# Dividing the x products anew over the eight steps of a block in a gated RNN kernel

## The chip, the cores and the metric

The kernel runs on one core of a Trainium2 chip. The metric is the device time of one execution in microseconds (us). PE is TensorE, DVE is VectorE, ACT is ScalarE, POOL is GpSimd and SP is SyncE; PEld is the part of TensorE that loads weights.

## What is computed

The reference is a gated recurrent cell over 512 time steps, with batch 8 and 512 units, all in float32, and the input added to the result:

```python
def step(h, x_t):
    fused = sigmoid(concatenate([x_t, h]) @ w_W + w_b)
    hidden_state, output_state = split(fused, 2)
    memory_state = x_t @ wx_W + wx_b + hidden_state * (h @ wh_W + wh_b)
    return output_state * h + (1.0 - output_state) * tanh(memory_state)
out = x + scan(step, cond, x)
```

Every step needs the h of the step before it. The products with x don't: they can be made ahead of time.

## The kernel before

**One step.** The loop over i (512 steps) writes out, in the order in which each engine will run them, all instructions of a step; no scheduler moves them. PE first runs the recurrent products of h with its weights. `ORDER` names them: A0 A1 A2 A3, then D0 to D3, then H2 H3. A letter is a PSUM tile (A has 256 columns for the first half of h and 192 for the second, D has 128, H has 64), a digit is a quarter of the 512 values of h. A0 and A1 read the first half of h (tile hTA), A2 and A3 the second (hTB). Each is a loop of four matmuls over j (the calls of `mm`, line 195). Such a matmul has 32 columns of weights (h or x of a few steps is the stationary operand) and writes to a strip of 32 partitions, so that four of them, one for each strip, run beside each other. A float32 matmul is two matmul instructions in the trace, each with its weight load. I call four matmul instructions on the four strips a **round**: a product of four matmuls is two rounds.

**The chain of a step.** When A is complete, DVE transposes its gate values (`tr`, L415; md1A, L430; `tz`, L415), ACT takes the sigmoids (L226), DVE runs a scan that makes the memory state (`m`, L403), ACT takes the tanh, and a second DVE scan writes the new h (`update`, L403), first for hTA, later for hTB. A0 of the next step waits for the first, A2 for the second.

**The x products.** After the recurrent products of step i, PE does one share of the x products of a later block: `take(later, 1)` resumes the generator `products(o)` until its next `yield`. A block o is eight steps, i = 8o to 8o + 7, and I write **u** for i modulo 8. The x products of two groups of four steps are made together with sums and differences of x and of the weights (p1, p2, p3, p4, p6, p7 and `shared`, after Strassen's way to multiply), from i = 4 on, and so for 62 blocks (o = 2 to 63). `pair(left, right, k, c0, c1)` is four matmuls of columns c0 to c1 of 384; `shared(k)` is four of 192 columns. The `yield` statements cut them into shares. There is none at the end of `products`, so that the last piece of one block and the first of the next are in one share. This is how columns fall on steps before the change:

| step u | pieces, in columns of four matmuls each | sum |
|---|---|---|
| 0 | 320 (p4, p3) | 320 |
| 1 | 64 (p4, p3), 192 (shared), 64 (p4, p3) | 320 |
| 2 | 192 (shared), 128 (p4, p3) | 320 |
| 3 | 192 (p4, p3), 128 (p1, p7 of the next block) | 320 |
| 4 | 256 (p1, p7), 64 (p1, p7) | 320 |
| 5 | 320 (p1, p7) | 320 |
| 6, 7 | 384 (p2, p6) | 384 |

**Beside it.** DVE and ACT also move the finished x products from PSUM (xp) to SBUF and into the start values of A, D and H, some work in each step after the updates (lines 526 to 585), and POOL adds x to the output (L595) and makes the sums of x (L294).

Of the kernel before, what the change touches and what calls it, by code (L numbers as in the profile page):

```python
# [48 lines left out]
def tile_cond_rnn_residual(  # L49
# [144 lines left out]
    def mm(out_, lhsT, rhs, start=False):  # L194
        nc.tensor.matmul(  # L195
            out_, lhsT, rhs, start=start, stop=False, skip_group_check=True
        )
# [69 lines left out]
    def wx_of(kh, nh):  # L267
        return wx[:, 2 * kh : 2 * kh + 2, 2 * nh : 2 * nh + 2]

    def x_half(o, n, kh):  # L270

        return x_of(o // 2, slice(2 * kh, 2 * kh + 2), 8 * (o % 2) + GS * n, GS)
# [23 lines left out]
    def products(o):  # L296

        t_ = [q[o % 2] for q in sx]
        p1 = (0, x_half(o, 0, 0), wx_of(0, 0))
        p2 = (0, x_half(o, 0, 1), wx_of(1, 0))  # L300
        p3 = (0, t_[3], wx_of(1, 1))
        p4 = (1, x_half(o, 1, 1), tw[3])
        p6 = (0, t_[1], tw[1])
        p7 = (1, t_[2], tw[2])

        def pair(left, right, k, c0=0, c1=WIDE):
            for j in range(NQ):
                bank, lhs, rhs = left if j < 2 else right
                mm(
                    xps[bank][32 * j : 32 * j + 32, COLS.start + c0 : COLS.start + c1],  # L310
                    lhs[:, k],
                    rhs[:, k, j % 2, c0:c1],
                    start=right is p7 and k == 0 and c0 == 0 and j >= 2,
                )

        def shared(k):
            for j in range(NQ):
                c0 = HALF * (1 - j // 2)
                mm(
                    xps[j // 2][32 * j : 32 * j + 32, COLS.start : COLS.start + HALF],  # L320
                    t_[0][:, k],
                    tw[0][:, k, j % 2, c0 : c0 + HALF],
                )

        pair(p1, p7, 0, 0, 128)
        if o > 2:
            yield
        pair(p1, p7, 0, 128)
        pair(p1, p7, 1, 0, 64)
        yield  # L330
        pair(p1, p7, 1, 64)
        yield
        pair(p2, p6, 0)
        yield
        pair(p2, p6, 1)
        yield
        pair(p4, p3, 0, 0, 320)
        yield
        pair(p4, p3, 0, 320)
        shared(0)  # L340
        pair(p4, p3, 1, 0, 64)
        yield
        shared(1)
        pair(p4, p3, 1, 64, 192)
        yield
        pair(p4, p3, 1, 192)

    def take(it, n=None):
        while n is None or n > 0:
# [4 lines left out]
    def x_side():  # L354
        for o in range(2, NG // 2):
            yield from products(o)
# [337 lines left out]
```

## Time and profile before

| | |
|---|---|
| median of 3 runs | 1657.46 us (1657.08 to 1657.48) |
| the profiled execution, its own time | 1659.18 us |
| its span, from the first to the last instruction | 1657.4 us |
| granted TensorE clock | 1.000 |
| PE busy | 1646.6 us (99%) |
| PEld busy | 1295.7 us (78%) |
| DVE busy | 1439.3 us (87%) |
| ACT busy | 1137.5 us (69%) |
| POOL busy | 328.5 us (20%) |

Matmuls are pipelined and the ends that the trace gives for them are modelled, so that a busy PE is not a PE without pauses: pauses of some tens of ns do not show as idle time. The starts are recorded. In the timeline a row is a group of like instructions: its start in us from the start of the span, its length in us, the engine, the line, the operation, the tile written and those read, the shape, and a count; behind it, in brackets, the idle time before it and what ended it.

### The profile page before, as it was taken

What the parts mean: (1) busy time and instruction counts of PE and PEld (TensorE: products, weight loads), DVE (VectorE), ACT (ScalarE), POOL (GpSimd) and SP (SyncE); (2) the same over time, 40 slices, a digit from 0 to 9 for tenths busy, and PEclk for the clock granted to TensorE, in tenths of its full rate; (3) what the DMA queues carried; (4) which work ended last, traced back from release to release, by engine and by line L of the source; (5) the groups of instructions that cost most, each with busy time, mean ns of one, the idle gap of its engine ahead of it and who ended that gap; (6) DMA issues with size and microseconds to landing.
All of it is one profiled execution on the core that took longest, in us unless ns stands there. A gap on an engine that the chain in (4) does not pass through costs nothing.

```text
span 1657.4 us, 114239 instructions
## 1 busy us (share of the span) xinstructions
PE 1646.6 (99%) x47566; PEld 1295.7 (78%) x47566; DVE 1439.3 (87%) x11237; ACT 1137.5 (69%) x5884; POOL 328.5 (20%) x1290
## 2 busy tenths in 40 slices
PE   9999999999999999999999999999999999999998
PEld 5778777787777777777877777778777777787776
DVE  6888888888888888888888888888888888888887
ACT  3667767677677676676776766767767667677665
POOL 2221121211211212112112121121121211211211
PEclk9999999999999999999999999999999999999999
DMA  4000000000000000000000000000000000000000
GB/s 180 17 5 17 17 17 17 10 11 17 17 17 17 5 17 17 17 17 4 18 17 17 17 13 9 17 18 17 17 5 18 17 17 17 4 17 10 11 11 10
DMA packets 11472, 30.41 MB, mean 18 GB/s; under 512 B 1220, under 2 KB 1732, under 8 KB 10952
## 3 DMA queue, kind: packets, MB, share of 16 engines
q1 hardware_dynamic: 10800, 22.94, 4.1%
q8 instruction: 372, 6.09, 1.6%
q14 instruction: 148, 1.21, 0.2%
q10 hardware_dynamic: 152, 0.16, 0.0%
HBM read 14.70 MB, written 8.39 MB: 14 GB/s over the span
## 4 chain that ended last, share of the span: by engine, by line
PE 97%; DVE 2%; issue 0%; ACT 0%; DVEq 0%
PE A L195 47%; PE D L195 26%; PE xp L195 18%; PE H L195 7%; DVE m L403 0%; DVE tr L415 0%; DVE md1B L472 0%; DVE tw L283 0%; DVE md1A L430 0%; DVE hTA L403 0%; DVE tz L415 0%; DVE hTA L167 0%; DVE hTB L167 0%; DVE hTB L403 0%; DVE md1B L430 0%
## 5 line engine op out<-in xcount | busy, mean ns | idle before, releaser
L195 PE MATMUL A<-wa,hTA 128*32 128x256 f32 x8176 | 535.6, 379 | 2.8 <-DVE hTA L403 2.7
L195 PE MATMUL A<-wa,hTB 128*32 128x192 f32 x8176 | 430.8, 328 | 0.0
L195 PEld LDWEIGHTS A<-wa,hTA 128*32 128x32 f32 x8176 | 270.0, 122 | 166.0 <-DVE hTA L403 81.6
L595 POOL TENSOR_TENSOR ot<-xin,hTB 128x16 f32<-128x16 f32 x503 | 125.1, 249 | 1287.6 <-DVE hTB L403 1276.9
L195 PEld LDWEIGHTS A<-wa,hTB 128*32 128x32 f32 x8176 | 258.1, 123 | 133.4 <-DVE hTB L403 103.5
L195 PE MATMUL D<-wd,hTB 128*32 128x128 f32 x8192 | 317.9, 273 | 0.0
L195 PE MATMUL D<-wd,hTA 128*32 128x128 f32 x8192 | 317.8, 273 | 0.0
L226 ACT ACTIVATE md0A<-tr 128x16 f32<-128x16 f32 x512 | 112.7, 220 | 242.0 <-DVE tr L415 229.6
L195 PE MATMUL xp<-tw,sx 128*32 128x192 f32 (+5 forms) x2480 | 276.3, 358 | 0.0
L195 PEld LDWEIGHTS D<-wd,hTA 128*32 128x32 f32 x8192 | 257.8, 122 | 20.8
L415 DVE STREAM_TRANSPOSE tr<-A 128x64 f32<-128x64 f32 x511 | 127.9, 250 | 147.6 <-PE A L195 138.6
L195 PEld LDWEIGHTS D<-wd,hTB 128*32 128x32 f32 x8192 | 240.7, 122 | 0.0
L226 ACT ACTIVATE hTB<-m 128x8 f32<-128x8 f32 x1024 | 163.4, 208 | 89.2 <-DVE m L403 85.7
L195 PE MATMUL xp<-wx,xin 128*32 128x384 f32 (+4 forms) x1552 | 219.2, 384 | 0.0
L195 PE MATMUL H<-wa,hTB 128*32 128x64 f32 x8192 | 208.5, 219 | 0.0
L195 PEld LDWEIGHTS H<-wa,hTB 128*32 128x32 f32 x8192 | 186.1, 122 | 0.0
L226 ACT ACTIVATE hTB<-hTB 128x16 f32<-128x16 f32 x512 | 121.1, 236 | 85.6 <-DVE hTB L403 84.7
L403 DVE TENSOR_TENSOR_SCAN hTA<-hd0A,hTA 128x24 f32<-128x24 f32 x1024 | 175.9, 172 | 0.0
L403 DVE TENSOR_TENSOR_SCAN hTB<-hd0B,hTB 128x24 f32<-128x24 f32 x1024 | 154.6, 193 | 21.8
L226 ACT ACTIVATE hTA<-m 128x8 f32<-128x8 f32 x1024 | 161.1, 206 | 2.3
L403 DVE TENSOR_TENSOR_SCAN m<-md0B,md1B 128x24 f32<-128x24 f32 x1024 | 154.7, 193 | 2.0
L403 DVE TENSOR_TENSOR_SCAN m<-md0A,md1A 128x16 f32<-128x16 f32 x1024 | 142.3, 181 | 8.6
(104 smaller groups left out, 2725.3 us busy)
## 6 DMA issues: line engine op xcount, KB each, us to landing
xin<-in_x_dram SPq DMA_DIRECT2D x31, 256.0 KB, 3.4
out_dram<-ot SPq DMA_DIRECT2D x31, 256.0 KB, 2.2
wx<-in_wx_dram SPq DMA_DIRECT2D x4, 768.0 KB, 7.0
wa<-in_wa_dram SPq DMA_DIRECT2D x4, 512.0 KB, 9.7
wd<-in_wd_dram SPq DMA_DIRECT2D x1, 768.0 KB
wd<-in_wd_dram SPq DMA_DIRECT2D x1, 256.0 KB, 11.2
out_dram<-ot SPq DMA_DIRECT2D x1, 192.0 KB, 3.3
head<-in_xh_dram ACTq DMA_DIRECT2D x1, 144.0 KB, 5.0
```

Of the source, the lines that this page charges most:

```text
L195: nc.tensor.matmul(out_, lhsT, rhs, start=start, stop=False, skip_group_check=True)
L226: inst = nc.scalar.activation(out_, in_, func, **kw).ins
L403: return nc.vector.tensor_tensor_scan(*[t_[:, :, c_].rearrange("p n c s -> p (n c s)") for t_ in (out_, d0, d1)], 0.0, ALU.mult, ALU.add,).ins
L415: inst = nc.vector.transpose(t_.rearrange("p c n -> p (c n)"), raw[n][hf]).ins
L595: return engine.tensor_tensor(ot[:, t, 2 * hf : 2 * hf + 2, :].rearrange("p c n -> p n c"), x_of(c, slice(2 * hf, 2 * hf + 2), t, 1).rearr ...
```

## The change

Only the widths at which four of the six pairs are cut are changed. No product is added or left out, no instruction is added, and the order of the pieces stays. The sums of columns by step, from u = 0 to 7, go from 320, 320, 320, 320, 320, 320, 384, 384 to 344, 304, 328, 304, 312, 328, 384, 384. The pieces of step 1 become 40, 192 and 72, those of step 2 become 192 and 136, those of step 3 become 176 and 128, those of step 4 become 256 and 56.

```diff
         pair(p1, p7, 0, 128)
-        pair(p1, p7, 1, 0, 64)
+        pair(p1, p7, 1, 0, 56)
         yield
-        pair(p1, p7, 1, 64)
+        pair(p1, p7, 1, 56)
         yield
         pair(p2, p6, 0)
         yield
         pair(p2, p6, 1)
         yield
-        pair(p4, p3, 0, 0, 320)
+        pair(p4, p3, 0, 0, 344)
         yield
-        pair(p4, p3, 0, 320)
+        pair(p4, p3, 0, 344)
         shared(0)
-        pair(p4, p3, 1, 0, 64)
+        pair(p4, p3, 1, 0, 72)
         yield
         shared(1)
-        pair(p4, p3, 1, 64, 192)
+        pair(p4, p3, 1, 72, 208)
         yield
-        pair(p4, p3, 1, 192)
+        pair(p4, p3, 1, 208)
```

## The prediction

> **What bounds the kernel now.** I read the head of the page and its chain of waits, then the groups of matmuls by shape, then the timeline of PE over one block of eight steps, and last the weight loads that wait for h.
>
> ```profile
> span 1657.4 us, 114239 instructions
> PE 97%; DVE 2%; issue 0%; ACT 0%; DVEq 0%
> ```
>
> The chain that ends last is PE in 97% of the span. So what counts is PE's stream, and pauses in it too short to show as idle time. Here is block 32 (steps 256 to 263), by the starts of its groups, with x products where they give a price:
>
> ```profile
> 838.23 1.05 PE L195 MATMUL A<-wa,hTA 128*32 128x256 f32 x16
> 839.75 0.62 PE L195 MATMUL D<-wd,hTA 128*32 128x128 f32 x16
> 840.62 0.41 PE L195 MATMUL H<-wa,hTB 128*32 128x64 f32 x16
> 840.84 0.44 PE L195 MATMUL xp<-tw,xin 128*32 128x320 f32 x2
> 841.11 0.44 PE L195 MATMUL xp<-tw,xin 128*32 128x320 f32 x2
> 841.38 1.04 PE L195 MATMUL A<-wa,hTA 128*32 128x256 f32 x16
> 842.94 0.62 PE L195 MATMUL D<-wd,hTA 128*32 128x128 f32 x16
> 844.58 1.05 PE L195 MATMUL A<-wa,hTA 128*32 128x256 f32 x16
> 845.45 0.83 PE L195 MATMUL A<-wa,hTB 128*32 128x192 f32 x16
> 846.10 0.62 PE L195 MATMUL D<-wd,hTA 128*32 128x128 f32 x16
> 847.74 1.05 PE L195 MATMUL A<-wa,hTA 128*32 128x256 f32 x16
> 849.27 0.62 PE L195 MATMUL D<-wd,hTA 128*32 128x128 f32 x16
> 850.91 1.05 PE L195 MATMUL A<-wa,hTA 128*32 128x256 f32 x16
> 854.06 1.05 PE L195 MATMUL A<-wa,hTA 128*32 128x256 f32 x16
> 857.21 1.05 PE L195 MATMUL A<-wa,hTA 128*32 128x256 f32 x16
> 858.74 0.62 PE L195 MATMUL D<-wd,hTA 128*32 128x128 f32 x16
> 860.48 1.05 PE L195 MATMUL A<-wa,hTA 128*32 128x256 f32 x16
> 863.74 0.83 PE L195 MATMUL A<-wa,hTA 128*32 128x256 f32 x12
> ```
>
> Two things are to be seen. First, a round's time goes by its columns: H is four rounds of 64 columns in 840.84 - 840.62 = 0.22 us, 55 ns each; 320 columns take 0.27 us a round. That is (270 - 55) / 256 = 0.84 ns a column and about 2 ns on top, and x columns are two rounds, so 1.67 ns for a column of a piece and 4 to 5 ns for a piece. Second, the part of a step from A0 to D0, in which no x product lies, isn't always the same: 1.52 us in step u = 0 (839.75 - 838.23) and u = 2, but 1.56 in u = 1, 1.53 in u = 3 and u = 6. The tile's durations give that excess in ns, one row for each of the windows of u = 1, 2, 3 and 6:
>
> ```profile
> L195 PE MATMUL A<-wa,hTB x16: 326/326/365, 842.2 to 842.8; 128*32 128x192 f32 x16
> L195 PE MATMUL A<-wa,hTB x16: 326/326/326, 845.4 to 846.0; 128*32 128x192 f32 x16
> L195 PE MATMUL A<-wa,hTB x16: 326/326/350, 848.6 to 849.1; 128*32 128x192 f32 x16
> L195 PE MATMUL A<-wa,hTB x16: 326/326/342, 858.1 to 858.6; 128*32 128x192 f32 x16
> ```
>
> The columns are the shortest, the median and the longest. The first round of A2 is stretched by 39 ns in u = 1, by 24 in u = 3 and by 16 in u = 6: PE pauses there, 79 ns in the 25.51 us of this block. What it waits for is in the rows of the weight loads:
>
> ```profile
> 842.25 0.51 PEld L195 LDWEIGHTS A<-wa,hTB 128*32 128x32 f32 x16 [0.29 <-DVE hTB L403]
> 845.38 0.54 PEld L195 LDWEIGHTS A<-wa,hTB 128*32 128x32 f32 x16 [0.22 <-DVE hTB L403]
> 848.58 0.51 PEld L195 LDWEIGHTS A<-wa,hTB 128*32 128x32 f32 x16 [0.27 <-DVE hTB L403]
> 851.71 0.53 PEld L195 LDWEIGHTS A<-wa,hTB 128*32 128x32 f32 x16 [0.22 <-DVE hTB L403]
> 854.86 0.53 PEld L195 LDWEIGHTS A<-wa,hTB 128*32 128x32 f32 x16 [0.22 <-DVE hTB L403]
> 858.05 0.51 PEld L195 LDWEIGHTS A<-wa,hTB 128*32 128x32 f32 x16 [0.26 <-DVE hTB L403]
> ```
>
> In every step the load of the second half of h waits for the DVE scan; mostly it is early enough. A2's slot is 0.87 us after A0 (845.45 - 844.58). In u = 1 the load starts exactly at the slot (842.25 = 841.38 + 0.87) and the pause is 39 ns, so the matmul follows the load by 40 ns, and the load must stand at A0 + 0.825 us or earlier. It stands 0.87 after A0 in u = 1, 0.84 in u = 3 and u = 6: late. It stands 0.80 in u = 2, 4 and 5: 20 to 30 ns to spare. Over the run:
>
> ```profile
> L195 PE MATMUL A<-wa,hTB 128*32 128x192 f32 x7536 | 396.6, 328 | 0.0
> ```
>
> The mean is 328 ns over 7536 instructions, four to a round, against 326: (328 - 326) x 7536 / 4 = 3.8 us of pauses between 100 and 1600 us (2.8 to 4.7 with the rounding), 0.064 us for each of 59 blocks, within reach of the 0.079 of the one that I read.
>
> **The change part by part.** The instructions of the two programs stand in the same order with the same count on every engine; only PE's widths differ. DVE, ACT, POOL and SP issue the same work, no DMA moves, and no semaphore wait is added. Sum of columns: 2688 a block before and after; pieces: 13 before and after. So PE's own work is the same, and the change can only move pauses. By 1.67 ns a column, A0 of the next step comes later by 24 columns = 40 ns after u = 0, by 13 after u = 2 and u = 5, earlier by 27 after u = 1 and u = 3, by 13 after u = 4. The chain to the next hTB starts at this step's own A and doesn't see the x products behind it, so a longer share moves the slot away from a late load, and a shorter one moves it towards it.
>
> - **u = 1 (39 ns now).** The share before it grows by 40 ns: pause 0 to 4.
> - **u = 3 (24 here).** u = 2 grows by 13: about 11 here. The mean of all blocks must be lower than this one (64 against 79): I take 5.
> - **u = 6 (16 here).** u = 5 grows by 13: 3.
> - **u = 2 (spare 25).** u = 1 gets shorter by 27, and its own pause of 39 goes as well, 66 in all. Is the load then 40 late? That depends on whether the chain of u = 1 starts earlier by the pause that has gone. Step 9 is also a u = 1, with a longer pause:
>
> ```profile
> 51.11 1.09 PE L195 MATMUL A<-wa,hTA 128*32 128x256 f32 x16
> 52.73 0.62 PE L195 MATMUL D<-wd,hTA 128*32 128x128 f32 x16
> 55.17 0.38 PEld L195 LDWEIGHTS A<-wa,hTB 128*32 128x32 f32 x12 [0.22 <-DVE hTB L403]
> ```
>
> D starts 1.62 after A0 there and the next load 4.06 after A0; in step 257 it is 1.56 and 4.00 (845.38 - 841.38). 60 ns more pause, 60 ns later: the chain follows the end of A. So 39 of the 66 cancel, 27 are used of a spare of 25: pause 0 to 4, and the upper bound, if the chain stays where it is, is about 38.
> - **u = 4 (spare 25).** u = 3 is shorter by 27, and its pause by 13 to 19, which cancels as above: 0 to 3.
> - **u = 5 (spare 25).** 13 used: nothing. u = 7 and u = 0 stand behind the shares of 384 and don't change.
> - **A0's own wait for hTA.** In u = 1 the four loads of A0 stood after the last x round; in the shorter steps they may begin with it, 0.05 us and more before A0, and the trace's shortest lead is 40 ns. Nothing.
> - **The narrow pieces.** No row shows a round under 64 columns. 40 columns by 0.84 ns are 36 ns a round, 56 are 49. If the matmul must follow its weight load by 40 ns also in a running stream, and the load starts with the round before it, a 40-column round takes 40 to 42 ns and delays the next load too: 6 to 12 ns a block. Lower bound 0 (the linear price; below it nothing speaks). Upper bound: 55 ns a round as for 64 columns, 2 x 19 + 2 x 6 = 50 ns a block. I take 9, near the lower end, since the 40 ns is a row about these very loads.
>
> A rule speaks for that upper bound. The Trainium skill, "TensorE: Matmul & The Clock Gate", section "Back-to-back issue gap", gives 1 to 64 columns one price, about 60 cycles, an issue floor of 25 ns. Read by columns, that would make the gain 0.7 us in place of 3.2. The trace doesn't bear the floor out for one matmul: H's 16 matmuls start within 0.22 us, 14 ns apart. The same page's section "LDWEIGHTS (loading the stationary operand)" gives columns / 1.2 ns for a load, 27 ns for 32 columns; by that a 40-column round is not held up, and the sum would be 3.8 us instead.
>
> **Sum.** Pauses now 76 a block (between 64 and 79, near the one that I read in ns), afterwards 4 + 2 + 5 + 1 + 3 = 15, so 61 less; minus 9 for narrow rounds is 52 ns. 62 blocks x 0.052 = 3.2 us. The profiled execution took 1659.18 us at a span of 1657.4; the unprofiled median is 1657.46. The steps are the same in both, so the difference carries over: 1657.46 - 3.2 = **1654.3 us**, 0.19% faster.
>
> **The rivals.**
>
> 1. *The chain takes the place of the pause.* The load for u = 2 stays at 4.00 us after A0 of u = 1, because another row than A's end holds the chain (DVE's extra work in u = 1, a scan that waits for ACT). Then u = 2 pauses 38 where u = 1 did: the gain is 61 - 34 - 9 = 18 ns a block, 1.1 us, 1656.3. If u = 4 does the same, it is nothing, 1657.6. Against it: step 9.
> 2. *Rounds under 64 columns cost what 64 cost.* The gain is 61 - 50 = 11 ns, 0.7 us, 1656.8. For it: no narrower round runs now. Against it: 40 ns from load to matmul is well under 55. The skill's row for 1 to 64 columns, weighed above, is this rule.
> 3. *Slower: weight loads set the pace of narrow rounds.* One pair of rows shows a matmul that took longer than its columns:
>
> ```profile
> 2.25 0.31 PE L195 MATMUL D<-none 128*128 128x128 bf16 x1
> 2.36 0.26 PE L195 MATMUL H<-none 128*128 128x64 bf16 x1
> 2.43 0.40 PE L195 MATMUL A<-none 128*128 128x256 bf16 x1
> ```
>
> 128 columns took 0.11 us until the next start, 64 took 0.07, not half. If a round of 40 and one of 56 cost 73 ns, four such rounds add 2 x 37 + 2 x 24 = 122 ns a block; against 61 saved that is 61 x 62 = 3.8 us, 1661.2. It is slower from 61 ns of added cost on. Against it: these loads have 128 columns and ours 32, and the 64-column rounds of H already run at 55.
> 4. *No narrow cost at all:* 1653.7, the lower end.
>
> That the change does something else than it says is excluded by the order of the programs.
>
> **How the numbers follow.** About 0.2%, 3.3 us, is what a measurement of this kernel can tell from no change. My forecast with its terms (gain 2.7 to 3.8 us): chance 0.66, with rival 4 as its far end; it straddles the bound, and just over half of it is on the near side, because 9 ns for the narrow rounds puts it there. Rival 1: 0.12. Rival 2: 0.12. Rival 3: 0.06. Left for what I don't see, either sign: 0.04. Faster by over 0.2%: 0.32 of the forecast's 0.66, nothing of rivals 1 and 2, and 0.02 of the rest, 0.34; slower 0.06 + 0.02 = 0.08; the remainder, 0.58, is within. The range goes from 1653.6 (no narrow cost, pauses all gone) to 1657.2 (rival 2 and most of rival 1); about 2 in 10 are left out.
>
> **What would show it.** In the profile after: the longest A<-wa,hTB matmul of u = 1 back at 326 to 330, of u = 3 and u = 6 at 326 to 335; the mean of its group 326 to 327; no new stretch in u = 2 or u = 4 (rival 1 would show 360 there). The distance between starts of the two 40-column rounds of u = 1: 36 to 42 ns (rival 2: 55, rival 3: 73). A block of 25.45 us instead of 25.50. I am wrong if the chain of u = 1 doesn't move with A's end, or if a row outside PE changes.

## The result and the profile after

The changed kernel takes 1654.87 us (median of 22 runs, 1654.60 to 1656.29) against 1657.44 us before (22 runs). The ratio is 0.9984, with a 95% interval of 0.9978 to 0.9991: 2.57 us or 0.16% faster. Predicted were 1654.3 us and 0.19%. The interval leaves out a ratio of 1, so 0.16% could be told from no change here, less than the 0.2% that the prediction took as the least.

The head of the page after, and its chain by engine:

```profile
span 1653.0 us, 114239 instructions
...
PE 97%; DVE 2%; DMA 1%; issue 0%; ACT 0%; DVEq 0%
```

PE sets the end as before. Rows of block 31 (steps 248 to 255) from the timeline of PE: A0 of u = 0 to 4, D0 of u = 0 to 2, and one half of the rounds of the narrow piece of u = 1:

```profile
809.98 1.05 PE L195 MATMUL A<-wa,hTA 128*32 128x256 f32 x16
811.50 0.62 PE L195 MATMUL D<-wd,hTA 128*32 128x128 f32 x16
813.17 1.05 PE L195 MATMUL A<-wa,hTA 128*32 128x256 f32 x16
814.68 0.62 PE L195 MATMUL D<-wd,hTA 128*32 128x128 f32 x16
815.78 0.20 PE L195 MATMUL xp<-tw,xin 128*32 128x40 f32 x2
815.82 0.21 PE L195 MATMUL xp<-tw,xin 128*32 128x40 f32 x2
816.30 1.05 PE L195 MATMUL A<-wa,hTA 128*32 128x256 f32 x16
817.83 0.62 PE L195 MATMUL D<-wd,hTA 128*32 128x128 f32 x16
819.48 1.05 PE L195 MATMUL A<-wa,hTA 128*32 128x256 f32 x16
822.61 1.05 PE L195 MATMUL A<-wa,hTA 128*32 128x256 f32 x16
```

From A0 to D0 it is now 1.51 us in u = 1 (814.68 - 813.17), where it was 1.56, and 1.53 in u = 2, where it was 1.52. The long pause has gone and a small one has come. In ns, by the durations of A<-wa,hTB (shortest, median, longest) in the windows of u = 1, 2, 3, 4 and 6 of this block:

```profile
L195 PE MATMUL A<-wa,hTB x16: 326/326/326, 814.0 to 814.5; 128*32 128x192 f32 x16
L195 PE MATMUL A<-wa,hTB x16: 326/326/337, 817.2 to 817.7; 128*32 128x192 f32 x16
L195 PE MATMUL A<-wa,hTB x16: 326/326/326, 820.3 to 820.9; 128*32 128x192 f32 x16
L195 PE MATMUL A<-wa,hTB x16: 326/326/337, 823.5 to 824.0; 128*32 128x192 f32 x16
L195 PE MATMUL A<-wa,hTB x16: 326/326/329, 829.8 to 830.3; 128*32 128x192 f32 x16
```

0, 11, 0, 11 and 3 ns. Blocks differ: in block 32, the one that the prediction read, u = 1 keeps 21 ns, and u = 2, 3, 4 and 6 have 2, 0, 6 and 11:

```profile
L195 PE MATMUL A<-wa,hTB x16: 326/326/347, 839.5 to 840.0; 128*32 128x192 f32 x16
```

That is an exception: by the starts, 54 of 59 steps of u = 1 pause for 2 ns or less. Over 100 to 1600 us the mean of this group fell from 328 to 327:

```profile
L195 PE MATMUL A<-wa,hTB 128*32 128x192 f32 x7544 | 394.3, 327 | 0.0
```

For means over many steps I use the recorded starts: the length of a block is A0 of step 488 less A0 of step 24, over 58 blocks; a pause is the mean time from A0 to D0 over 59 steps of the same u, less 1513.4 ns, which is this mean in u = 0, 5 and 7, where PE doesn't pause. Here are the two ends for the profile before, for a second profile of the kernel before (a run described below) and for the changed kernel, each kernel's two rows in a fence of its own:

```profile
99.03 1.05 PE L195 MATMUL A<-wa,hTA 128*32 128x256 f32 x16
...
1577.70 1.05 PE L195 MATMUL A<-wa,hTA 128*32 128x256 f32 x16
```

```profile
97.69 1.05 PE L195 MATMUL A<-wa,hTA 128*32 128x256 f32 x16
...
1575.81 1.04 PE L195 MATMUL A<-wa,hTA 128*32 128x256 f32 x16
```

```profile
97.60 1.05 PE L195 MATMUL A<-wa,hTA 128*32 128x256 f32 x16
...
1573.40 1.05 PE L195 MATMUL A<-wa,hTA 128*32 128x256 f32 x16
```

That is 25.494, 25.485 and 25.445 us a block. All kernels, in ns, the sum over all eight u:

| kernel | block | pause u = 1, 2, 3, 4, 6 | sum |
|---|---|---|---|
| before, first profile | 25494 | 40, 0, 15, 0, 15 | 69 |
| before, second profile | 25485 | 38, 0, 6, 0, 15 | 59 |
| the change | 25445 | 1, 9, 1, 4, 5 | 20 |
| the change, two more profiles | 25447, 25451 | 1 to 2, 9 to 10, 0 to 2, 4 to 7, 5 to 6 | 21, 25 |
| u = 0 and 1 alone (p1_alone) | 25470 | 1, 23, 7, 0, 15 | 45 |
| u = 2 and 3 alone (p2_alone) | 25479 | 35, 0, 0, 3, 16 | 54 |
| u = 4 and 5 alone (p3_alone) | 25473 | 37, 0, 7, 0, 3 | 47 |
| over | 25481 | 1, 48, 0, 3, 4 | 55 |
| relieve | 25487 | 37, 0, 8, 0, 17 | 61 |
| relieve_div | 25438 | 5, 2, 1, 0, 4 | 13 |
| trim | 25437 | 1, 5, 1, 1, 4 | 11 |
| best | 25440 | 3, 1, 3, 2, 5 | 14 |

In every row the block less its pauses is 25425 to 25426 ns: PE's own work, which the change doesn't touch. The time went out of the pauses. (In best and in one of the "two more profiles" a single step of u = 3 pauses for 110 and 92 ns, which makes up about 2 ns of its sum; why is open.)

### The profile page after: what moved, and what is told of

Same layout as the page of the kernel before. It is cut to its first block, busy times and chain, and to the rows that moved or that the text cites. A ratio compares the mean times of both kernels' runs of the same rounds, so it can differ in the third digit from the quotient of the medians.

```text
span 1653.0 us, 114239 instructions
## 1 busy us (share of the span) xinstructions
PE 1640.8 (99%) x47566; PEld 1291.2 (78%) x47566; DVE 1438.5 (87%) x11237; ACT 1136.4 (69%) x5884; POOL 328.7 (20%) x1290
## 4 chain that ended last, share of the span: by engine, by line
PE 97%; DVE 2%; DMA 1%; issue 0%; ACT 0%; DVEq 0%
PE A L195 47%; PE D L195 26%; PE xp L195 17%; PE H L195 7%; DMA wd<-in_wd_dram 1%; DVE m L403 0%; DVE tr L415 0%; DMA rows<-in_bias_dram 0%; DVE md1B L472 0%; DVE tw L283 0%; DVE md1A L430 0%; DVE hTA L403 0%; DVE tz L415 0%; DVE hTB L403 0%; DVE md1B L430 0%
```

## The experiments

My theory: PE never rests but for pauses in front of A2, whose weight load waits for the second half of h; the division moves A2's slot against that load and nothing else, and the chain to the next load follows the end of A. Rivals: the chain doesn't follow, so that a pause only moves on; narrow rounds are dear; the gain has another source.

**Three of the four moved cuts, one at a time.** The change moves four cuts, which lie in three of the six pairs. Each edit here is against the kernel before, and blocks are compared with its second profile:

```diff
-        pair(p4, p3, 0, 0, 320)
+        pair(p4, p3, 0, 0, 344)
...
-        pair(p4, p3, 0, 320)
+        pair(p4, p3, 0, 344)
```

> Step u = 0 gets 344 columns, u = 1 gets 40 + 192 + 64 = 296, all others as before. Pauses theory (only the pauses in front of A2 change, and the chain follows the end of A): the pause of u = 1 goes from 41 ns to 0 to 2; u = 2, whose slot comes 40 + 41 earlier while its chain starts 41 earlier, gets a pause of about 15; u = 3 keeps 0 to 18 and u = 6 its 14. A block saves 28 to 46 ns, the kernel 1.7 to 2.9 us, 1654.6 to 1655.7. Rival, the chain stays where it is: the pause of u = 2 is 55, nothing is saved, 1657.4. Rival, narrow rounds are dear: the two 40-column rounds of u = 1 start 55 ns apart or more and A0 of u = 2 is later by that.

Measured: 1656.64 us against 1657.30 beside it (ratio 0.9997, interval 0.9988 to 1.0006), 14 ns a block. Two windows of A<-wa,hTB, of u = 1 and u = 2 in block 31:

```profile
L195 PE MATMUL A<-wa,hTB x16: 326/326/327, 814.8 to 815.3; 128*32 128x192 f32 x16
L195 PE MATMUL A<-wa,hTB x16: 326/326/347, 817.9 to 818.4; 128*32 128x192 f32 x16
```

The 24 columns take the pause of u = 1 away wholly, as expected, and u = 2 gets one: 23 ns in the mean, where I expected 15 and the rival 55. The chain follows the end of A, but lands some 8 ns later than that. The time saved missed its range (0.7 us for 1.7 to 2.9), because I counted from the 69 to 76 ns of the first profile and not from the 59 of the second, and by these 8 ns.

```diff
-        pair(p4, p3, 1, 64, 192)
+        pair(p4, p3, 1, 64, 208)
...
-        pair(p4, p3, 1, 192)
+        pair(p4, p3, 1, 208)
```

> Only the cut between u = 2 and u = 3 is moved: u = 2 gets 192 + 144 = 336, u = 3 gets 176 + 128 = 304. No round is under 64 columns. Pauses theory: u = 1 keeps its 41 ns, the pause of u = 3 (18 before) goes to 0, u = 4 gets 0 to 5, u = 6 keeps 14: 13 to 18 ns a block, 0.8 to 1.1 us, 1656.3 to 1656.6. Rival, columns moved change nothing: 1657.4.

Measured: 1657.05 us (0.9998, 0.9989 to 1.0007), 6 ns a block and not 13 to 18, so that the time missed its range too. The pause of u = 3 is 0, and u = 4 has 3. The pause that it takes away was 15 in the first profile of before, from which I had the 18, but it is 6 to 8 in the four others with the same pieces in u = 2 and 3 (before again, p1_alone, p3_alone, relieve). And 3 of the 6 ns lie in u = 1, which this cut doesn't touch.

```diff
-        pair(p1, p7, 1, 0, 64)
+        pair(p1, p7, 1, 0, 56)
...
-        pair(p1, p7, 1, 64)
+        pair(p1, p7, 1, 56)
```

> Only the cut between u = 4 and u = 5 is moved: 256 + 56 and 328. Pauses theory: the pause of u = 6 goes from 14 to 16 ns to 2 to 4, u = 5 stays without one: 11 ns a block, 0.7 us, 1656.7. Rival, narrow rounds are dear (the 56-column rounds at 55 ns or more in place of 49): 1656.9 to 1657.4, and the starts of these two rounds show it.

Measured: 1656.50 us (0.9995, 0.9986 to 1.0004), 12 ns a block; the pause of u = 6 is 3. As the pauses theory has it. Its two rounds of 56 columns start 49 ns apart in each of 58 blocks (49 to 50), the price by columns and not the rival's 55.

None of the intervals of these three runs can tell its kernel from the one before; the pauses in the traces do.

The three save 14 + 6 + 12 = 32 ns of the whole's 40. The rest fits the fourth cut, from 64 to 72, which was not run alone: with it u = 1 keeps 304 columns and not the 296 of p1_alone, A2's slot in u = 2 comes 13 ns later, and its pause is 9 and not 23.

**Too much of it.** 24 columns more from u = 1 to u = 2 in the changed kernel:

```diff
-        pair(p4, p3, 1, 0, 72)
+        pair(p4, p3, 1, 0, 48)
...
-        pair(p4, p3, 1, 72, 208)
+        pair(p4, p3, 1, 48, 208)
```

> The changed kernel with 24 more columns moved from u = 1 to u = 2: u = 1 has 40 + 192 + 48 = 280, u = 2 has 192 + 160 = 352. Pauses theory: the slot of u = 2 comes 40 ns earlier, its pause rises from about 8 to 41 to 48, u = 3 loses its last ns; 27 to 33 ns a block more than the changed kernel, 1.7 to 2.0 us, 1656.6 to 1656.9. Rival, the gain of the change doesn't come from these pauses: as the changed kernel, 1654.9, since all columns are there and no piece is added.

Measured: 1657.39 us against 1657.30 (1.0002, 0.9993 to 1.0010): the whole gain is gone, with the same columns and as many pieces. A block is 36 ns longer than the changed kernel's (27 to 33 expected), and the time lies over its range. The window of u = 2 in block 31:

```profile
L195 PE MATMUL A<-wa,hTB x16: 325/326/367, 818.6 to 819.2; 128*32 128x192 f32 x16
```

The slot was moved by 40 ns, and the mean pause grew by 39, from 9 to 48. The gain of the change comes from these pauses: the rival that seeks it elsewhere falls.

**The late h itself.** Instead of moving columns, I tried to make h of u = 0 earlier, with the widths of before:

```diff
-                nc.scalar.copy(u2[Q23], xps[0][Q23, COLS])
+                inst = nc.scalar.copy(u2[Q23], xps[0][Q23, COLS]).ins
+                tc.add_manual_dep(inst, spread_d.name, SYNC)
```

(`spread_d` is the copy into D of u = 5.)

> The kernel before with its widths, but in u = 0 the sigmoid that makes sz no longer carries a second wait (on ACT itself): the copy that makes u2 in u = 7 waits for that instruction's source instead, long after it is done. Theory: h of the second half is late in u = 0 because sz starts 0.14 us later there than in the other steps; without that, sz starts at 3.04 us after A0 as elsewhere, the load for A2 of u = 1 comes 20 to 50 ns earlier, the pause of u = 1 falls from 41 to 0 to 20 ns without moving a column, 1.2 to 2.5 us less, 1654.9 to 1656.2. Rival, the pause of u = 1 has to do with the x products of u = 0 and not with the late h: nothing changes, 1657.4.

Measured: 1657.29 against 1657.46 us (0.9998, 0.9989 to 1.0007), the pause of u = 1 is 37. ACT in u = 0 of block 31, whose A0 starts at 811.44:

```profile
811.44 1.05 PE L195 MATMUL A<-wa,hTA 128*32 128x256 f32 x16
```

```profile
814.36 0.23 ACT L226 ACTIVATE md0B<-tr 128x16 f32<-128x16 f32 x1
814.62 0.22 ACT L226 ACTIVATE sz<-D 128x64 f32<-128x64 f32 x1
```

The second wait of sz is gone from this trace, but sz still starts 3.18 us after A0, behind the end of the sigmoid before it. So that wait isn't what holds it back; this edit missed its aim, and the late h was not tested this way. Why sz is late in u = 0 stays open.

**Better divisions.** Three kernels with other cuts, against the changed kernel; relieve_div and best also carry the edit of relieve. The pair behind a cut starts where the pair before it ends (208 becomes 204 in all three).

```diff
 # trim: 344, 308, 320, 308, 312, 328, 384, 384
-        pair(p4, p3, 1, 0, 72)
+        pair(p4, p3, 1, 0, 76)
...
-        pair(p4, p3, 1, 72, 208)
+        pair(p4, p3, 1, 76, 204)
 # relieve_div: 336, 312, 324, 308, 312, 328, 384, 384
-        pair(p4, p3, 0, 0, 344)
+        pair(p4, p3, 0, 0, 336)
...
-        pair(p4, p3, 1, 72, 208)
+        pair(p4, p3, 1, 72, 204)
 # best: 340, 312, 320, 308, 312, 328, 384, 384
-        pair(p4, p3, 0, 0, 344)
+        pair(p4, p3, 0, 0, 340)
...
-        pair(p4, p3, 1, 72, 208)
+        pair(p4, p3, 1, 76, 204)
```

> The changed kernel with its largest remaining pause treated: u = 1 gets 4 columns more (40 + 192 + 76 = 308), u = 2 gets 320, u = 3 gets 180 + 128 = 308. Pauses theory: u = 2 from 8 to about 3, u = 4 from 4 to 1, u = 3 between 0 and 18 by whether its chain is quick as in the changed kernel or slow as before: between 0.6 us less and 0.4 us more than the changed kernel, 1654.3 to 1655.3. Rival, these last ns are noise of the phases and not of the widths: as the changed kernel.

> The same removal of the second wait, with widths cut for it: 336, 48 + 192 + 72 = 312, 192 + 132 = 324, 180 + 128 = 308, 312, 328, 384, 384. Pauses theory: 0 to 2 in u = 1 and u = 2, 0 to 11 in u = 3, 1 in u = 4, 4 in u = 6; 6 to 17 ns a block against about 20 in the changed kernel, 0.2 to 0.9 us below it, 1654.0 to 1654.7. Rival, the changed kernel is already at the floor of PE's own work: 1654.9.

> The changed kernel once more, beside the others on the same chip: 1654.9. Its profile is a second look at its pauses: about 20 ns a block in all, the largest in u = 2.

Measured beside each other, against 1657.46 us for the kernel before: trim 1654.66 (0.9982, 0.9973 to 0.9991), relieve_div 1654.21 (0.9981, 0.9972 to 0.9990), the changed kernel 1655.03 (0.9984, 0.9975 to 0.9993). trim and relieve_div lie in the ranges of the pauses theory. Their blocks are 10 and 9 ns shorter than the changed kernel's beside them, 0.5 to 0.6 us over 62, where the medians differ by 0.37 and 0.82. Of what relieve_div has beyond its blocks, some 0.15 us lie behind the x products: from A0 of step 499 to the end the three kernels with the edit of relieve take 44.4 to 44.5 us, all others 44.6 to 44.7.

> The two divisions that beat the changed kernel put together: 340, 44 + 192 + 76 = 312, 192 + 128 = 320, 180 + 128 = 308, 312, 328, 384, 384, and the wait of sz taken off as in the two kernels that had it. Pauses theory, from the pauses that those two showed (u = 1 has 1 ns at a share of 344 and 6 at 336; u = 2 has 6 behind a share of 308 and 2 behind 312): 2 to 3, 2, 2, 1 and 4 ns, 11 a block against 14 to 16, 0.2 to 0.3 us below the quicker of them, 1653.9 to 1654.2. Rival, 14 ns is the floor that the phases leave: 1654.2 to 1654.7.

> The changed kernel beside it, once more: 1654.8 to 1655.1, and about 23 ns of pauses a block.

Measured: best 1654.84 against 1657.72 us (0.9981, 0.9972 to 0.9990), the changed kernel beside it 1655.42 (0.9984, 0.9975 to 0.9993), with pauses of 25 ns. Both times lie over their ranges, and the kernel before is 0.26 us slower here than beside trim. Best has 14 ns of pauses, no fewer than the two that it joins: by its pauses the rival was right. These three divisions leave 11 to 14 ns. All three beat both kernels by the medians beside them and by their blocks; the intervals of the ratios overlap with the changed kernel's.

**The price of a narrow round, by itself.** In the changed kernel the pieces of u = 6 and u = 7 are cut:

```diff
-        pair(p2, p6, 0)
+        for n in range(8):
+            pair(p2, p6, 0, 40 * n, 40 * n + 40)
+        for n in range(4):
+            pair(p2, p6, 0, 320 + 16 * n, 336 + 16 * n)
...
-        pair(p2, p6, 1)
+        for n in range(16):
+            pair(p2, p6, 1, 24 * n, 24 * n + 24)
```

> The changed kernel with the 384 columns of u = 6 cut into eight pieces of 40 and four of 16, and those of u = 7 into sixteen of 24; nothing else. It prices a narrow round by itself. By columns alone: starts of the rounds 36, 16 and 22 ns apart, u = 6 longer by 11 x 5 = 55 ns, u = 7 by 75. If a matmul follows its weight load by 40 ns and the load starts with the round before: never under 40 ns a round, u = 6 longer by 16 x 4 + 8 x 24 + 55 = 310 or so, u = 7 by 32 x 18 + 75 = 650. If rounds under 64 columns cost what 64 cost: 55 ns each.

Measured in one run: 1908 us, 251 more than before, far over every case. The first 40-column rounds of u = 6 (wx,xin is one half of a round):

```profile
962.56 0.21 PE L195 MATMUL xp<-wx,xin 128*32 128x40 f32 x2
962.59 0.21 PE L195 MATMUL xp<-wx,xin 128*32 128x40 f32 x2
962.63 0.21 PE L195 MATMUL xp<-wx,xin 128*32 128x40 f32 x2
962.66 0.21 PE L195 MATMUL xp<-wx,xin 128*32 128x40 f32 x2
962.70 0.21 PE L195 MATMUL xp<-wx,xin 128*32 128x40 f32 x2
962.73 0.21 PE L195 MATMUL xp<-wx,xin 128*32 128x40 f32 x2
962.77 0.21 PE L195 MATMUL xp<-wx,xin 128*32 128x40 f32 x2
962.80 0.21 PE L195 MATMUL xp<-wx,xin 128*32 128x40 f32 x2
```

Eight rounds in a row, 0.24 us from the first to the eighth: 34 to 35 ns each, the price by columns, without the 40 ns from load to matmul and far from 55. In the changed kernel itself the two rounds of 40 columns stand 0.04 apart in block 31 (815.78, 815.82), and 35 ns in each of 58 blocks; those of 56 columns stand 49 ns apart. So the narrow rounds of the change cost nothing extra, as the equal blocks without pauses in the table also say. The Trainium skill, "TensorE: Matmul & The Clock Gate", section "Back-to-back issue gap", gives 1 to 64 columns one price; the trace doesn't agree, a round of 40 costs 35 ns here where one of 64 costs 55. Where most of the 251 us went, stands in the last section.

**The kernel before, again.**

> The kernel before once more, for a second profile: the first had an execution of 1659.2 us where the median is 1657.4. If its 1.7 us more lie in the start, steps 4 to 499 take the same here; the pauses of u = 1, 3 and 6 again 41, 18 and 15 ns in the mean.

Measured: 1657.23 us, near the median. A0 of step 4 starts at 33.06 us in it and at 34.36 in the first profile; from step 20 to step 499 it takes 1525.9 us and the first profile 1526.5. So of 1.9 us between the two executions 1.3 lie in the start, but 0.6 lie in the blocks, against what I expected: the pause of u = 3 is 6, where 18 were expected and the first profile has 15 in the mean.

## Why the prediction was right

- **What bounds the kernel:** right. PE without rest but for the pauses in front of A2, as over shows and the equal blocks without pauses in the table.
- **The pauses before: mis-sized.** I took 76 ns a block, near the one block that I had read in ns. The mean of that profile is 69, and a second profile, of an execution near the median, has 59. "The steps are the same in both, so the difference carries over" failed: the pauses vary from one execution to the next, u = 3 most, and the quoted execution was 1.7 us over the median. The mean of the group (64) was the better row, and was in hand.
- **u = 1, 3 and 6:** right. 4, 5 and 3 were forecast, 1, 1 and 5 measured.
- **u = 2 and u = 4: mis-sized.** Forecast 2 and 1, measured 9 and 4. The chain follows the end of A, so that rival 1 (38 ns in u = 2) falls, but not to the ns: the load for u = 2 came 3.99 us after A0 of u = 1 in the mean of the first profile, 3.95 by my rule without the pause of 40 ns, and 3.96 is the mean of the changed kernel. With a spare of 25 and 27 used, these ten ns are a pause.
- **Narrow rounds: mis-sized.** 9 ns forecast, none measured (35 ns for 40 columns, 49 for 56). Rivals 2 and 3 fall with it; the row that rival 3 leaned on, of weights with 128 columns, doesn't hold for 32.
- **The sum:** forecast 76 - 15 - 9 = 52 ns, measured 59 - 20 = 39, and 40 by the blocks (25485 - 25445). 62 x 0.040 = 2.5 us, where the medians give 2.57. Two errors of 17 and 5 ns made the forecast too large and one of 9 too small; together they are 13 ns or 0.8 us by this sum, and 0.6 us of it is between 1654.3 and 1654.9. That the total came so near is in part luck: a price that isn't there, 9 ns for narrow rounds, made up for half of pauses that were put too high. The gain of 2.57 us lies just under the 2.7 to 3.8 to which I gave a chance of 0.66, far over those of rivals 1 and 2 (1.1 and 0.7).

## What to carry to other kernels

Where one engine is busy all the time, look for pauses in its starts: the same stretch of work, compared over the steps of a period, and the longest against the median duration of the group that waits. Fill-in work is then best divided by where each step's late input falls, not evenly; what a step gives up has to come out of a spare that is measured, and what goes beyond it comes back as a pause (40 ns as 39, in over). For gains of this size read the base from two profiles, or from a mean over the run, and never from one block.

## What the runs showed of the hardware

- Very many narrow matmuls outrun their instructions. In narrow, the 24-column rounds of u = 7 take about 33 ns (65 matmuls start within 0.535 us), not the 22 that columns would give, and then PE stops for over 2 us with nothing that it waits for in the profile:

```profile
967.36 0.19 PE L195 MATMUL xp<-tw,sx 128*32 128x24 f32 x1
969.68 0.21 PE L195 MATMUL xp<-tw,sx 128*32 128x24 f32 x1 [2.13 <-issue]
```

  Its waits named "issue" add up to 142 us on PE:

```profile
PE xp L195 <- issue: 86.2, 77, 2.4
PE A L195 <- issue: 33.8, 31, 2.3
PE D L195 <- issue: 15.0, 25, 1.3
PE H L195 <- issue: 6.8, 14, 1.1
```

  The columns are the total in us, the times and the longest. The trace shows what comes late. Queue q8 (kind: instruction) brings 16 KB at a time; its rows in the pages of the kernel before and of narrow (packets, MB, share) are:

```profile
q8 instruction: 372, 6.09, 1.6%
```

```profile
q8 instruction: 472, 7.73, 1.7%
```

  PE has 60462 matmuls in narrow against 47566, each with a weight load, and that is about 256 instructions to a packet in both kernels. In narrow the packets never start less than 3.3 us apart, while 256 instructions are 32 narrow rounds, about 1.1 us at 33 ns. Each of the 107 stops of PE over 0.7 us after the first 50 us, 155 us in all, ends 1.2 to 1.6 us after a packet has landed; of moments picked at random, 11% lie so. So it is the supply of instructions that gives out, though no run varied it. What makes up the other 96 us was not taken apart.
- The pauses of one and the same program differ between executions: 69 and 59 ns a block before, 20 to 25 after. What sets them isn't known from these runs.
